# Channel attention: ten 32 x 32 diagonal blocks with tokens on partitions in place of eight, on one Trainium2 core

## The chip, the cores and the metric

The kernel runs on one core of a Trainium2 chip. The metric is the device time of one execution in microseconds (us). A core has a matrix engine (TensorE, "PE" in the profile, with its weight loads as "PEld"), a vector engine (DVE), a scalar engine (ACT), a general engine (POOL) and a queue engine for transfers (SP). Each runs its own instructions strictly in order and waits for the others by semaphores: an instruction that has to wait holds back everything behind it on its engine.

## The reference, cut to what matters

The input has 8 x 1024 tokens of 256 numbers. The first layer is an attention over the *channels* of one token: every token has 16 heads of 64 channels, and the score of channel q against channel k is the product of two numbers.

```python
Q = (x @ Wq + bq).reshape(b, s, H, C) * inv_sqrt_c      # H = 16, C = 64
K = (x @ Wk + bk).reshape(b, s, H, C)
V = (x @ Wv + bv).reshape(b, s, H, C)
scores = jnp.einsum('bshq,bshk->bshqk', Q, K)           # 64 x 64 for each token and head
scores = jnp.where(mask, -inf, scores)                  # mask: k > q
w = jax.nn.softmax(scores, axis=-1)
attn = jnp.einsum('bshqk,bshk->bshq', w, V)
x = layernorm(x + attn.reshape(b, s, 1024) @ Wo + bo)
```

A second layer (an ordinary attention over positions and a mixture of experts) follows. The change doesn't touch it.

## The kernel before, in words

`phase_a` holds the first layer. The 8192 tokens are cut into 64 tiles of 128 (t = 0 to 63), and the loop body of a tile has eight steps, c = 0 to 7. Step c treats four heads (g = c % 4) for one half of the tile's tokens (ww = c // 4). The order of all instructions is written out by hand (`manual_schedule`), in the loop and in five tables (`head`, `fill_a`, `middle`, `between`, `fill_b`) that say which side job is put at which place of which step.

The 64 x 64 triangle of a head is cut into an upper 32 x 32 triangle, a lower one and a full square between them. There are two ways to compute them.

- **On TensorE.** `scores(t, c, which)` forms the products with matmuls into PSUM tiles `pair` (L418), the mask being added by a matmul with `sel` and `late` (L407). ACT takes the exponential into an `e` tile (L433). `sums(t, c, which)` multiplies `e` with the values `V`, which also hold a column of ones, into the PSUM tile `sum` (L453, L463), and ACT copies that into `S` (L479), from where POOL's transfers bring it into `nd` (L489). `which` 0 and 1 are the upper triangle with the square, 64 columns for each head, `which` 2 is the lower triangle, 32 columns.
- **With tokens on partitions.** For the channels `own` = T0 to T0 + TC, DVE multiplies (`token_scores`, L536), POOL subtracts the row's maximum (`token_less`, L544), ACT takes the exponential (`token_exp`, L550, L553), DVE weighs with the values and adds up (`token_weigh`, L561, L563, L564; `token_sums`, L573). A triangle is halved again and again: squares of 16 (parts A and B), 8 (part C), 4, 2, 1 and the diagonal (part F). `invert(t, 1)` adds the results to `nd` (L584, L589) and takes the reciprocal (L590); `divide` multiplies (L594). Before the change these channels are those of heads 6 to 9: both triangles of four heads, eight blocks. TensorE computes only the square of these heads.

Other places that the steps below speak of:

- `proj_k`, `proj_q`, `proj_v` (L288, L330, L299): the projections of the next tile, at steps 0 and 1, 2 and 3, 4 and 5. They write the PSUM tile `ps`, which has one buffer: TensorE can't start a projection before DVE has read the last one (L289, L331, L306). The reads are called k0, k1, q0, q1, v0, v1 here.
- `sum` has one PSUM buffer too: the matmuls of a `sums` wait until ACT has emptied the one before. `pair` has three.
- `token_v` (L497) transposes values into the right half of `ps` at step 6; `output` puts the product with `Wo` into its left half (L632) at steps 6 and 7; DVE adds the residual (`r`, L637). `token_v_out` (L502) is ACT's copy of the transposed values into `vt`. It stands at step 7, ahead of the S copy of `sums(t, 6, "inner")`, and its semaphore is that of DVE's `r`.
- `build` issues the transfers into `R` and `L` (L370 on POOL, L376 on SP). `gather` is a small memset on POOL (L384, "event") that waits for them, and the matmuls of `scores` wait for the memset. On POOL it stands behind `token_less` of parts A and B at step 1, and behind that of part C at step 5. `token_less` A is made to wait for DVE's scans of the next tile (`extrema`, L342, L344).
- `spread_v` (L320) lays the values out for TensorE.
- The transfer `nd<-S` after step 2 (L489, on POOL's queue) waits until DVE's `divide(t, 1)` has read `nd`.

Of the kernel before, what the change touches and what calls it, by code (L numbers as in the profile page):

```python
# [165 lines left out]
def phase_a(tc, a, ident, x1_d, norm_scalars, share, view):  # L166
# [11 lines left out]
    HT = 4  # L178
    TC = HT * C1
    T0 = (H1 - HT) // 2 * C1  # L180
    own = slice(T0, T0 + TC)
    levels = {"A": [(16, 0, 4)], "B": [(16, 4, 4)], "C": [(8, 0, 16)], "F": [(4, 0, 32), (2, 0, 64), (1, 0, 128), (0, 0, 256)]}
    inner = {1: (2, 3), 2: (0, 1)}
    chunk = [0, 1, 2, 5, 6, 7, 3, 4]
    slot = {c: s for s, c in enumerate(chunk)}
    with (
# [29 lines left out]
        for to, of, n in ((0, 0, 3), (3, 5, 3), (6, 3, 2)):  # L216
            nc.scalar.dma_start(bv[:, to : to + n], bv_c[:, of : of + n], allow_slow_non_contiguous=True)
# [22 lines left out]
        for n, big in (("hi", 3e38), ("lo", -3e38)):  # L240
            lim[n] = wp.tile([P, HH], FP, name=f"lim_{n}")
# [11 lines left out]
        NV = 2 * H1 - HT  # L253
# [21 lines left out]
        nc.gpsimd.memset(Ss[1][:, :, :2, 0:32], 0.0)  # L275
# [37 lines left out]
        def spread_v(t, ww, half):  # L313

            src = state["vT", t].rearrange("p i (w u a b) -> p i w u a b", w=2, u=4, a=4)
            for qd in (2 * half, 2 * half + 1):
                at, n = (H1, (H1 - HT) // 2) if qd % 2 else (0, H1 // 2)
                V = Vs[ww][:, at : at + 2 * n].rearrange("p (i r) u (a b) -> p i r u a b", r=2, a=4)
                for aa in range(4):
                    nc.vector.tensor_copy(  # L320
                        V[32 * aa : 32 * aa + 32, :, qd // 2, :, aa, 0:4],
# [67 lines left out]
        def scores(t, c, which):  # L389
# [6 lines left out]
            heads = range(2 * which, 2 * which + 2) if which < 2 else range(4)  # L396
            n = 64 if which < 2 else 32
            g = c % 4
            free = inner.get(g, ()) if which == 2 else ()
            at = 0 if which < 2 or 0 not in free else 256  # L400
            width = 256 if free else 512
            masked = [h for h in heads if h not in free]
            for x, h in sorted(enumerate(heads), key=lambda xh: xh[1] not in free):
                if h == masked[0]:
                    for u in range(4):
                        pr = slice(32 * u, 32 * u + 32)
                        nc.tensor.matmul(  # L407
                            bank[u][:, at : at + width].rearrange("p (n i) -> p n i", i=n)[:, :, 0:32],
                            sel[pr].rearrange("p a j -> p (a j)"),
                            late[pr, None, :].to_broadcast([32, width // n, 32]),  # L410
# [4 lines left out]
                jb = 0 if which < 2 or h in free else 1  # L415
                for u in range(4):
                    pr = slice(32 * u, 32 * u + 32)
                    one = nc.tensor.matmul(  # L418
                        bank[u][:, x * 4 * n : (x + 1) * 4 * n].rearrange("p (b i) -> p b i", i=n),
                        Lt[pr, 2 * (h0 + h) + jb].rearrange("p a j -> p (a j)"),  # L420
                        R[pr, :, h0 + h, 64 - n :],
                        start=h in free,
                        stop=h in free or h == masked[-1],
# [8 lines left out]
            for i in range(2):  # L432
                nc.scalar.activation(es[i], pair[i], AF.Exp)  # L433
# [1296 lines left out]
```

## Time and profile before

| what | value |
|---|---|
| median of 3 runs | 4629.45 us (4629.16 to 4637.17) |
| the profiled execution, its own time | 4629.18 us |
| its span, first to last instruction | 4627.5 us |
| mean granted TensorE clock | 0.979 |
| the 64 tiles of `phase_a` | 57 to 3850 us of the span |
| one tile, from one `turn` (L603) to the next, 2003.80 to 2063.04 us | 59.24 us |
| DVE busy over the span | 3708.1 us (80%) |
| ACT busy over the span | 3563.6 us (77%) |
| POOL busy over the span | 3353.0 us (72%) |

Busy time of an engine includes time in which nobody waits for it. A line of the timeline has the start, the duration, the engine, the line of the kernel, the operation, what it writes and reads, how many instructions are merged in it, and in brackets how long its engine was idle before it and what ended that. Matmuls overlap; the time that a group of them takes on TensorE is read from its start to the start of the next group.

### The profile page before, as it was taken

How to read it: one execution, taken by the hardware profiler on the slowest of the kernel's cores; microseconds unless marked ns; L12 is line 12 of the kernel's file. 1: busy time of each engine (PE TensorE's matmuls, PEld its weight loads, DVE VectorE, ACT ScalarE, POOL GpSimd, SP SyncE). 2: the span in 40 equal slices, each digit the busy share in tenths (PEclk: the TensorE clock that was granted, in tenths of full speed). 3: DMA queues.
4: the chain of work that ended last, by engine and by line, in shares of the span. 5: the costliest groups of instructions: out<-in, count | busy, mean ns of one | idle time of the engine just before them, and what ended most of it. 6: DMA issues, size and time to landing. Idle time of an engine off the chain costs nothing.

```text
span 4627.5 us, 169371 instructions
## 1 busy us (share of the span) xinstructions
PE 4381.9 (95%) x70232; PEld 2971.7 (64%) x70232; DVE 3708.1 (80%) x6686; ACT 3563.6 (77%) x5015; POOL 3353.0 (72%) x5672
## 2 busy tenths in 40 slices
PE   7999999999999999999999999999999998888785
PEld 4666666666666666666666666666666665555563
DVE  6888888888888888888888888888888885677778
ACT  5888888888888888888888888888888885444344
POOL 6878887887788788778877887888788784133446
PEclk9999999999999999999999999999999999999897
DMA  2222222222222222222222222222222222232553
GB/s 81 53 50 55 51 53 52 54 53 53 52 53 55 52 55 54 52 53 51 53 52 54 53 53 53 53 54 54 52 54 53 52 51 70 59 80 70 142 160 115
DMA packets 521272, 285.66 MB, mean 62 GB/s; under 512 B 373425, under 2 KB 439345, under 8 KB 520497
## 3 DMA queue, kind: packets, MB, share of 16 engines
q1 hardware_dynamic: 378466, 113.23, 12.5%
q0 software_dynamic: 139264, 159.69, 11.1%
q8 instruction: 550, 9.01, 0.8%
q10 hardware_dynamic: 2768, 1.91, 0.2%
q14 instruction: 224, 1.84, 0.1%
HBM read 72.84 MB, written 33.85 MB: 23 GB/s over the span
## 4 chain that ended last, share of the span: by engine, by line
PE 66%; DVE 14%; POOL 5%; SPq 5%; issue 4%; DMA 3%; ACT 3%; POOLq 0%; DVEq 0%; ACTq 0%
PE pair L418 19%; PE sum L453 12%; PE sum L463 8%; PE ps L299 6%; PE pair L407 5%; PE ps L330 5%; SPq L376 4%; PE ps L632 4%; DVE s L564 2%; POOL s L544 2%; DMA L<-k 2%; PE ps L288 2%; PE pair L603 1%; ACT s L1044 1%; DVE V L320 1%
## 5 line engine op out<-in xcount | busy, mean ns | idle before, releaser
L433 ACT ACTIVATE e<-pair 128x1024 f32<-128x1024 f32 x2560 | 2482.0, 1022 | 508.3 <-PE pair L418 477.0
L418 PE MATMUL pair<-R,L 32*128 32x128 f32 (+1 forms) x28672 | 1401.7, 319 | 22.0 <-POOL event L384 20.3
L489 POOL DMA_DIRECT2D nd<-S x2048 | 973.1, 483 | 517.0 <-ACT e L433 351.8
L418 PEld LDWEIGHTS pair<-R,L 32*128 32x128 f32 x28672 | 1096.7, 186 | 139.2 <-POOL event L384 75.4
L370 POOL DMA_DIRECT2D R<-qm x2048 | 988.6, 490 | 9.9 <-issue 5.0
L453 PE MATMUL sum<-e,V 128*32 128x256 f32 x12288 | 965.4, 386 | 5.9 <-ACT S L479 5.6
L463 PE MATMUL sum<-e,V 128*32 128x128 f32 x16384 | 783.1, 274 | 0.2 <-ACT S L479 0.2
L463 PEld LDWEIGHTS sum<-e,V 128*32 128x32 f32 x16384 | 496.2, 110 | 404.3 <-ACT e L433 96.2
L544 POOL TENSOR_TENSOR s<-s,qm 128x1024 f32<-128x1024 f32 (+2 forms) x320 | 486.9, 1537 | 132.3 <-DVE lo L344 129.0
L479 ACT COPY S<-sum 128x512 f32<-128x512 f32 (+1 forms) x1024 | 551.8, 539 | 37.0 <-PE sum L463 37.0
L320 DVE COPY V<-vT 32x128 f32<-32x128 f32 (+1 forms) x2048 | 449.3, 219 | 26.2
L590 DVE RECIPROCAL att<-nd 128x384 f32<-128x384 f32 (+1 forms) x192 | 438.0, 2281 | 12.5 <-DMA nd<-S 10.1
L564 DVE TENSOR_TENSOR s<-s,vt 128x1024 f32<-128x1024 f32 (+2 forms) x320 | 409.7, 1280 | 11.1
L76 POOL TENSOR_SCALAR ve<-mv 128x1 f32<-128x1 f32 x128 | 85.0, 664 | 449.6 <-DVE mv L74 431.6
L453 PEld LDWEIGHTS sum<-e,V 128*32 128x32 f32 x12288 | 305.1, 109 | 154.2 <-issue 64.4
L407 PE MATMUL pair<-late,sel 32*128 32x256 bf16 (+1 forms) x5120 | 399.3, 298 | 4.0 <-ACT e L433 4.0
L306 DVE TENSOR_TENSOR vT<-ps,bv 128x512 f32<-128x512 f32 x128 | 87.7, 685 | 342.9 <-PE ps L299 342.9
L536 DVE TENSOR_TENSOR s<-k,qm 128x1024 f32<-128x1024 f32 (+2 forms) x320 | 324.5, 1031 | 0.0
L563 DVE TENSOR_REDUCE part<-s 128x64 f32<-128x1024 f32 (+3 forms) x320 | 301.8, 943 | 8.3 <-ACT s L550 8.3
L299 PE MATMUL ps<-xT,wv 128*128 128x128 f32 x2048 | 273.0, 289 | 25.6 <-DVE qm L331 24.8
L299 PEld LDWEIGHTS ps<-xT,wv 128*128 128x128 f32 x2048 | 248.2, 198 | 69.0 <-issue 38.5
L573 DVE TENSOR_REDUCE part<-s 128x64 f32<-128x1024 f32 (+3 forms) x320 | 287.9, 932 | 2.2
(253 smaller groups left out, 5673.9 us busy)
## 6 DMA issues: line engine op xcount, KB each, us to landing
R<-qm POOLq DMA_DIRECT2D x2048, 32.0 KB, 2.0
nd<-S POOLq DMA_DIRECT2D x2048, 32.0 KB, 1.9
L<-k SPq DMA_DIRECT2D x4088, 8.0 KB
rows_d<-yx SPq DMA_DIRECT2D x32, 512.0 KB
xT<-in_xT SPq DMA_DIRECT2D x64, 128.0 KB
xr<-in_x SPq DMA_DIRECT2D x64, 128.0 KB
x_d<-x1o SPq DMA_DIRECT2D x64, 128.0 KB
w<-in_w SPq DMA_DIRECT2D x32, 256.0 KB
```

The costliest lines, as they stand in the source:

```text
L299: nc.tensor.matmul(ps[:, i * P : (i + 1) * P], w["v"][:, c, chunk[ch] * P : (chunk[ch] + 1) * P], xT_of[t][:, c, :], start=c == 0, stop=c ...
L320: nc.vector.tensor_copy(V[32 * aa : 32 * aa + 32, :, qd // 2, :, aa, 0:4], src[32 * qd : 32 * qd + 32, :n, ww, :, aa, :],)
L370: moved.append((None, nc.gpsimd.dma_start(R[:, b, s, b, :], q[:, b, s, cols])))
L407: nc.tensor.matmul(bank[u][:, at : at + width].rearrange("p (n i) -> p n i", i=n)[:, :, 0:32], sel[pr].rearrange("p a j -> p (a j)"), late ...
L418: one = nc.tensor.matmul(bank[u][:, x * 4 * n : (x + 1) * 4 * n].rearrange("p (b i) -> p b i", i=n), Lt[pr, 2 * (h0 + h) + jb].rearrange(" ...
L433: nc.scalar.activation(es[i], pair[i], AF.Exp)
L453: nc.tensor.matmul(dst[32 * u : 32 * u + 32], Vs[ww][:, v, u, :], e[u // 2][:, u % 2, x * 256 : (x + 1) * 256].rearrange("p (b i) -> p b i ...
L463: nc.tensor.matmul(dst[32 * u : 32 * u + 32], Vs[ww][:, v if alone else H1 + v, u, :], e2[u // 2][:, u % 2, h * P : (h + 1) * P].rearrange ...
L479: nc.scalar.copy(S[:, :, at : at + 2, i0:].rearrange("p b h i -> p h b i"), ps[:, : 8 * (C1 - i0)].rearrange("p (h b i) -> p h b i", h=2, ...
L489: nc.gpsimd.dma_start(tok[:, b, s, (h0 - G) * C1 : (h0 + G) * C1], Sx[:, 4 if s else b, b, :])
L544: one = nc.gpsimd.tensor_tensor(s, s, m, ALU.subtract)
L564: nc.vector.tensor_tensor(s, s, v[:, :, None, :].to_broadcast([P, nb, w, w]), ALU.mult)
```

## The change

Two more blocks are computed with tokens on partitions: the lower triangle of head 5 and the upper triangle of head 10. `own` is now channels 352 to 671 (TC = 320, not 256). On TensorE head 5 loses its lower triangle, and head 10 only keeps its square and its lower triangle. Which blocks a call of `scores` and `sums` treats is read from the table `plan`. Since the two heads of a `sums` can now have different widths, its copy into `S` is made in two pieces where they do.

Two of the ten blocks lie in other rows of the transposed values than the eight did, so `token_v_more` transposes two strips of 32 columns more, into the unused right half of the `sum` tile of step 6, with two copies by ACT behind it. To make room in memory, `vt` and `xr` now have one buffer (pool `op`) where they had two (`xp`), and the limits of the scans (`lim`) are of 16 bits.

```diff
-    HT = 4
-    TC = HT * C1
-    T0 = (H1 - HT) // 2 * C1
+    T0, TC = 352, 320
     own = slice(T0, T0 + TC)
-    levels = {"A": [(16, 0, 4)], "B": [(16, 4, 4)], "C": [(8, 0, 16)], "F": [(4, 0, 32), (2, 0, 64), (1, 0, 128), (0, 0, 256)]}
+    nb = TC // 32
+    levels = {
+        "A": [(16, 0, nb // 2)],
+        "B": [(16, nb // 2, nb // 2)],
+        "C": [(8, 0, 2 * nb)],
+        "F": [(4, 0, 4 * nb), (2, 0, 8 * nb), (1, 0, 16 * nb), (0, 0, TC)],
+    }
+    both_heads = ((0, 0, 64, True), (1, 0, 64, True))
+    last_heads = ((2, 0, 64, True), (3, 0, 64, True))
+    whole = {0: both_heads, 1: last_heads, 2: tuple((h, 1, 32, True) for h in range(4))}
+    plan = {
+        0: whole,
+        1: {0: both_heads, 2: ((0, 1, 32, True), (2, 0, 32, False), (3, 0, 32, False))},
+        2: {
+            1: ((2, 0, 32, False), (3, 0, 64, True)),
+            2: ((0, 0, 32, False), (1, 0, 32, False), (2, 1, 32, True), (3, 1, 32, True)),
+        },
+        3: whole,
+    }
     inner = {1: (2, 3), 2: (0, 1)}
-    chunk = [0, 1, 2, 5, 6, 7, 3, 4]
+    chunk = [0, 1, 5, 6, 7, 2, 3, 4]
...
-            lim[n] = wp.tile([P, HH], FP, name=f"lim_{n}")
+            lim[n] = wp.tile([P, HH], BF, name=f"lim_{n}")
...
             es = spare.pop(0)
             for i in range(2):
-                nc.scalar.activation(es[i], pair[i], AF.Exp)
-            state["e", t, c, which] = es
+                nc.scalar.activation(es[i][:, :, :at], pair[i][:, :, :at], AF.Exp)
+            state["e", t, c, which] = es, starts
...
-            nc.scalar.copy(
-                S[:, :, at : at + 2, i0:].rearrange("p b h i -> p h b i"),
-                ps[:, : 8 * (C1 - i0)].rearrange("p (h b i) -> p h b i", h=2, b=4),
-            )
+            to = G * (g % 2) + heads[0]
+            pieces = [(0, 2)] if spans[0][1] == spans[1][1] else [(0, 1), (1, 1)]
+            for x, nh in pieces:
+                start, width = spans[x]
+                nc.scalar.copy(
+                    S[:, :, to + x : to + x + nh, C1 - width :].rearrange("p b h i -> p h b i"),
+                    ps[:, start : start + 4 * nh * width].rearrange("p (h b i) -> p h b i", h=nh, b=4),
+                )
+            if alone and c == 6 and t + 1 < NT:
+                token_v_more(t + 1, ps, 2 * P)
...
-            n = TC // P
-            for i in range(n):
-                nc.tensor.transpose(ps[:, (2 + i) * P : (3 + i) * P], state["vT", t][:, HID // P - n + i, :], ident)
-            state["vt", t] = xp.tile([P, TC], FP, name="vt")
+            for i in range(2):
+                nc.tensor.transpose(ps[:, (2 + i) * P : (3 + i) * P], state["vT", t][:, HID // P - 2 + i, :], ident)
+            state["vt", t] = op.tile([P, TC], FP, name="vt")
             state["pv", t] = ps
 
+        def token_v_more(t, ps, at):
+
+            for x, (ch, r) in enumerate(((2, slice(96, 128)), (5, slice(0, 32)))):
+                nc.tensor.matmul(
+                    ps[:, at + 32 * x : at + 32 * x + 32],
+                    state["vT", t][:, slot[ch], :],
+                    ident[:, r],
+                    start=True,
+                    stop=True,
+                )
+            for x in range(2):
+                nc.scalar.copy(
+                    state["vt", t][:, (TC - 32) * x : (TC - 32) * x + 32], ps[:, at + 32 * x : at + 32 * x + 32]
+                )
+
         def token_v_out(t):
-            nc.scalar.copy(state["vt", t], state["pv", t][:, 2 * P : 2 * P + TC])
+            nc.scalar.copy(state["vt", t][:, 32 : TC - 32], state["pv", t][:, 2 * P :])
...
-            xr = xp.tile([P, D], FP, name="xr")
+            xr = op.tile([P, D], FP, name="xr")
```

In the built program the first matmul of `token_v_more` waits on ACT's semaphore for the S copy of the same `sums` call, and the copy `token_v_out` still waits for DVE's `r`. The order of the jobs in the five tables is unchanged.

More of the change, by code (lines that the diff above doesn't have):

```diff
@@ L395, in scores @@
             bank = [pair[u // 2][:, u % 2, :] for u in range(4)]
[L396 to L403, printed above, removed]
+            work = plan[c % 4][which]
+            n = max(w[2] for w in work)
+            starts, at = {}, 0
+            for h, jb, m, mask in work:
+                starts[h] = at
+                at += 4 * m
+            fill = [starts[w[0]] for w in work if w[3]]
+            masked = [w[0] for w in work if w[3]]
+            a0, a1 = fill[0], fill[-1] + 4 * n
+            for h, jb, m, mask in sorted(work, key=lambda w: w[3]):
                 if h == masked[0]:
@@ L414, in scores @@
                         )
-                jb = 0 if which < 2 or h in free else 1
                 for u in range(4):
@@ L837, in phase_a @@
         token_v(0, pps.tile([P, 512], FP, name="ps"))
+        token_v_more(0, state["pv", 0], 0)
         token_v_out(0)
```

67 lines of the change are left out of this document (29 added, 38 removed).

## The prediction

> **What bounds the kernel now.** I read the page's busy line and slices first, then the list of waits, then the timelines of one tile engine by engine.
>
> ```profile
> PE 4381.9 (95%) x70232; PEld 2971.7 (64%) x70232; DVE 3708.1 (80%) x6686; ACT 3563.6 (77%) x5015; POOL 3353.0 (72%) x5672
> PE   7999999999999999999999999999999998888785
> ```
>
> In the slices of the 64 tiles TensorE has no gap: a tile costs the 59.24 us of its matmuls. The list of waits (who waits, for whom: us in total, times, longest) shows how near the others are:
>
> ```profile
> DVE vT L306 <- PE ps L299: 342.9, 67, 6.3
> DVE k L289 <- PE ps L288: 236.5, 63, 4.0
> ACT vt L502 <- DVE r L637: 35.8, 62, 1.3
> ```
>
> DVE has slack at two places only, 5.4 us a tile before v1 and 3.7 us before k1. Between these it works without a pause, and at `r` ACT already waits for it in nearly every tile. DVE's timeline from v1 to `r`:
>
> ```profile
> 2010.65 0.69 DVE L306 TENSOR_TENSOR vT<-ps,bv 128x512 f32<-128x512 f32 x1 [4.11 <-PE ps L299]
> ...
> 2020.22 1.22 DVE L564 TENSOR_TENSOR s<-s,vt 128x1024 f32<-128x1024 f32 x1
> 2021.48 1.22 DVE L573 TENSOR_REDUCE part<-s 128x128 f32<-128x1024 f32 x1
> 2022.80 0.43 DVE L637 TENSOR_TENSOR r<-ps,xr 128x256 f32<-128x256 f32 x1
> ```
>
> All engines around that place:
>
> ```profile
> 2022.62 0.65 PE L463 MATMUL sum<-e,V 128*32 128x128 f32 x16
> 2023.20 0.29 PE L407 MATMUL pair<-late,sel 32*128 32x256 bf16 x4
> 2023.26 0.37 ACT L502 COPY vt<-ps 128x256 f32<-128x256 f32 x1 [0.45 <-DVE r L637]
> 2023.53 0.38 ACT L479 COPY S<-sum 128x256 f32<-128x256 f32 x1
> 2024.29 0.64 PE L453 MATMUL sum<-e,V 128*32 128x256 f32 x8
> ```
>
> TensorE goes from the inner sums straight to the next scores at 2023.20. ACT empties `sum` meanwhile, by 2023.91, and TensorE wants it again at 2024.29. Two more places without slack, from the timelines of POOL, PE and DVE:
>
> ```profile
> 2039.65 0.09 POOL L384 MEMSET event<- 1x1 f32 x1
> 2039.80 0.73 PE L418 MATMUL pair<-R,L 32*128 32x128 f32 x16 [0.16 <-POOL event L384]
> 2048.76 0.69 DVE L331 SCALAR_TENSOR_TENSOR qm<-ps,bias 128x512 f32<-128x512 f32 x1
> 2049.77 1.98 PE L330 MATMUL ps<-wq,xT 128*128 128x512 f32 x4
> ```
>
> The event comes when the scores of step 2 need it, and q0 is read 0.4 us before TensorE wants `ps` for q1.
>
> **What TensorE saves.** From starts of groups in the timeline: the sums of one head take 0.46 us with 256 columns (2018.17 to 2018.63) and 0.22 us with 128; the scores of two heads with 256 take 0.97 us (0.485 each), of four with 128 0.99 us (0.25 each); four mask matmuls take 0.22 us with 512 columns, 0.12 with 256, so about 0.06 with 128. For half a tile, head 5 loses one scores block and part of a mask (0.25 + 0.06 = 0.31) and one sums block (0.22); head 10 goes from 256 to 128 columns: 0.235 + 0.06 = 0.30 in scores, 0.24 in sums. That is 1.07 us, 2.14 us a tile. `token_v_more` adds two matmuls, four records in the profile's way of counting: at 0.12 us each as with the 128x128 weights of `proj_v` (16 in 1.98 us) 0.5 us, as the two transposes L497 (0.27 us together) 0.27; I take 0.4. ACT gains about as much as it loses: eight exponentials get 256 elements shorter (1059 ns at 1024, 845 at 768 in L550's rows: 0.21 us each, 1.7 us), against 0.9 us for parts A, B, C and F, 0.1 for split copies and some 0.5 for two small ones.
>
> **What DVE and POOL get.** Rows by form: a reduction takes 1210, 676 and 407 ns with 1024, 512 and 256 elements, a product 681, 419 and 286 with 512, 256 and 128: 1.04 ns an element. So an instruction on part A, B or C (1024 to 1280) gets 0.27 us longer, one on 512 elements 0.13, on 256 0.07, on 128 0.03. POOL's subtraction (1945, 1124 and 728 ns) gets 0.41 us longer on A, B or C. Reciprocals: 2545 ns for 384, 1753 for 256, 6.2 ns an element; the two outer ones get 0.2 us shorter, the inner one 0.4 longer. In all some 5.6 us more on DVE in a tile, on 48.9 busy (3128 us in 64 tiles); below 59, so DVE isn't the bound by its sum. What counts is where it falls.
>
> **The path, step by step** ("+" is later than in the tile shown, with v1 as zero).
> 1. From v1 to `r`: weighing F 0.13 + 0.07 + 0.13 + 0.07 + 0.03 + 0.07 = 0.50, weighing and summing C 3 x 0.27 = 0.80, the spread -0.03: 1.27 us. DVE waited 0.1 us here before `r` (0.29 on average: 18.3 us over 64 tiles), so `r` is 1.1 late and ends at 2024.33.
> 2. The new matmuls sit behind the S copy, this one behind the copy into `vt`, and that behind `r`. 2024.33 + 0.03 + 0.27 (start of L502 to start of the copy) + 0.38 + 0.05 for the handover = 2025.06; plus 0.4 for the matmuls themselves: TensorE takes up the scores of step 7 at 2025.46, not 2023.20: +2.26. What it had saved since v1 (0.22 + 0.30 + 0.24) is spent waiting.
> 3. Step 1 saves 0.31: k1 at +1.95. DVE reaches the scans at +1.1 + 0.54 (scores A, B) - 0.24 (reciprocal, division) = +1.4, POOL's A and B add 0.82: the event at +2.2. The scores of step 2 start at +2.2.
> 4. From k1 to q0 DVE has more: sums F 0.20, the additions to `nd` 0.13 + 5 x 0.07, reciprocals 0.2, division 0.05: 0.93. q0's read ends at 2049.36 + 1.95 + 0.93 = 2052.24. TensorE would be ready for q1 at 2049.77 + 2.2 - 0.22 - 0.30 - 0.24 = 2051.21; it starts at 2052.3: +2.5.
> 5. Scores F 0.30, weighing A and B 4 x 0.27: q1's read ends at 2056.64 + 4.25 = 2060.9, as v0 wants `ps` at 2061.0. Step 5 saves 0.31: v1 at **+2.2 us**. DVE (sums A, B and scores C: +5.0) is through its scans at 2069.6 and waits for v1 at 2072.0, so step 1 starts afresh in every tile.
>
> The event of step 6 is covered: POOL's transfers `nd<-S` wait for the division (+2.88), F adds 0.45 and C 0.41: the event, at 2069.12 in the next tile, comes at 2072.9, 0.9 us too late for its scores (2069.79 + 2.2), but TensorE would stand before the new matmuls in that time anyway; with that cover gone it would cost 0.9. The single buffers cost nothing: `vt` is overwritten by a copy that waits for `r`, behind its last reader on DVE, and `xr` is loaded at step 2, 25 us after `r` has read the last one (SP's queue then holds no transfer up). The 16-bit limits lie between no gain and 0.5 us a scan (from 1.21 us to the 0.68 us of a product of that size); I take none, since TensorE comes to the event at +1.95 anyway.
>
> The sum: `token_v_more` stands in the loop 63 times, 63 x 2.2 = 139; 4629.2 + 139 = 4768 us. The profiled execution (4629.18) is the median's (4629.45). This case's own ends: without the stalls of steps 3 and 4, 2.26 - 1.38 (all that TensorE saves behind the stall) = 0.88 us a tile, 4685; with weighing A and B slowed by POOL (L564's mean is 1582 ns against 1.22 us alone, twice 0.36 before q1), 0.4 more in step 1 and 0.1 in step 2, 3.4 us a tile, 4843.
>
> **Rivals.** *The clock drops (slower still).* TensorE stands still once a tile, from 2022.44 (2023.20 - 0.76) to 2025.06, 2.6 us, less what step 6's event takes of it: 1.7 to 2.6 us. The windows of the trace (span, busy times by engine, granted clock, transfers):
>
> ```profile
> 3980.00:3982.50 2.50, 0.00 (x0) 0.00 (x0) 0.27 (x2) 2.50 (x15) 0.00 (x0) 1.00 0.01 3
> 3865.00:3867.50 2.50, 1.94 (x20) 1.40 (x12) 2.43 (x7) 0.88 (x1) 0.00 (x0) 0.50 0.00 0
> ```
>
> A gap of 2.97 us (ended 3982.69) left the clock at 1.00; one of 2.16 us among tiny matmuls (ended 3864.07) was followed by 7 us at about half, some 3.4 us lost. In a tile 1.4 of these would go into stalls that steps 3 and 4 charge anyway, so 2 us: 4768 + 126 = 4894 if in every tile, 4810 in a third. Against it: the gap is 0.4 us or more shorter than the harmless one. The Trainium skill, "TensorE: Matmul & The Clock Gate", section "Why this matters for your kernels", warns of idle gaps above about 3 us between bursts, after which the clock halves. By it the gap is harmless and the sum stays 4768; by the row at 3865 it need not be.
>
> *TensorE goes on setting the time (faster).* For it: 95% busy, idle time on the others. If DVE were not late at `r`, a tile would cost 1.16 (step 2 without lateness) - 1.38 = -0.22 us, 4615; with the wait of the new matmuls hidden too, -2.14 + 0.4 = -1.74 us, 4520. It decides from a lateness below 0.22 us; against it are 1.27 us of work on an engine that had 0.1 to 0.3 us there.
>
> *A balance.* Lateness near 0.2 us: no change.
>
> **How the numbers follow.** The path 0.75 (4685 to 4843), the clock 0.15 (4800 to 4900), TensorE 0.07, balance 0.03. Three runs agree within 0.2%, about what a measurement here can tell from no change (9 us). Predicted 4768, range 4685 to 4880; faster 0.07, same 0.03, slower 0.90.
>
> **What would show it.** In the changed profile: TensorE idle 1.7 to 2.6 us a tile, released by the S copy at step 7; ACT's wait for `r` up from 0.6 to above 1 us a tile; a tile of 61 to 62 us; TensorE waiting for DVE before q1; DVE still waiting before v1. Wrong would be: no idle time of TensorE at step 7, a tile under 59 us, or a clock below 1 within the tiles.

## The result, and the profile after

| | before | changed |
|---|---|---|
| time, us (medians of the runs compared) | 4629.89 | 5005.35 (4992.07 to 5028.6, 4 runs) |
| ratio, with its 95% interval | 1 | 1.0813 (1.077 to 1.0855) |
| predicted, us | | 4768 (4685 to 4880) |
| mean granted clock of the profiled run | 0.979 | 0.956 |
| a tile from v1 to v1, median (mean), us | 59.23 (59.99) | 65.07 (65.79) |
| of it v1 to `r` | 12.15 (12.35) | 15.55 (15.53) |
| `r` to k1 | 16.87 (16.79) | 18.12 (18.79) |
| k1 to v1 | 30.21 (30.85) | 30.65 (31.47) |

The kernel got slower as predicted, but by 375 us instead of 139, which is beyond the predicted range. The last four rows come from the timelines of DVE: the starts of its reads v1, `r` and k1, and the medians of their distances, with the means over 61 tiles in brackets (medians of parts need not add up to that of the whole; the means do). From the first v1 to the last the profiled run takes 354 us longer than the one before (4127.8 and 3773.9), of 363 for the whole span, so the tiles hold the loss. The profiled run of the changed kernel took 4992.07 us. Its busy line:

```profile
PE 4438.5 (89%) x68440; PEld 2985.4 (60%) x68440; DVE 4106.3 (82%) x6686; ACT 3517.0 (70%) x5271; POOL 3553.9 (71%) x5672
```

Records of TensorE fell by 1792 and its busy time rose, so the records got longer on average. DVE's instructions are as many as before, and their busy time rose by 398 us: 6.2 us a tile, where the prediction had 5.6; but 2.0 of the 6.2 are one product that has only 0.13 us more to do, as is seen below. The list of waits (who waits, for whom: us in total, times, longest):

```profile
DVE vT L322 <- PE ps L315: 209.7, 66, 5.5
...
PE pair L435 <- POOL event L400: 115.8, 57, 3.7
...
PE sum L517 <- ACT S L491: 106.0, 63, 3.4
...
ACT vt L530 <- DVE r L665: 88.4, 62, 3.2
PE ps L346 <- DVE qm L347: 83.0, 62, 1.4
```

TensorE now stands still in three places of a tile: before the scores that need POOL's event (2.0 us each; 20.3 us in all before), before the new matmuls (1.7 us, in every tile) and before q1 (1.3 us). DVE still waits before v1, 3.2 us a tile. Where v1 to `r` grew is seen in the timeline of one tile, DVE and POOL together (start, duration, engine, line):

```profile
2048.63 2.42 POOL L572 TENSOR_TENSOR s<-s,qm 128x1280 f32<-128x1280 f32 x1
2048.93 0.69 DVE L322 TENSOR_TENSOR vT<-ps,bv 128x512 f32<-128x512 f32 x1 [2.97 <-PE ps L315]
2049.54 0.81 DVE L591 TENSOR_REDUCE part<-s 128x160 f32<-128x640 f32 x1
2050.38 4.52 DVE L592 TENSOR_TENSOR s<-s,vt 128x640 f32<-128x640 f32 x1
2050.98 0.09 POOL L400 MEMSET event<- 1x1 f32 x1
2051.03 1.27 POOL L368 TENSOR_TENSOR qm<-qm 128x512 f32<-128x512 f32 x1
2052.25 1.27 POOL L369 TENSOR_TENSOR lo<-lo,qm 128x512 f32<-128x512 f32 x1
2053.48 0.72 POOL L641 TENSOR_TENSOR xr<-xr,bo 128x256 f32<-128x256 f32 x1
...
2065.47 0.41 DVE L665 TENSOR_TENSOR r<-ps,xr 128x256 f32<-128x256 f32 x1
```

The first product of weighing F (L592) takes 4.52 us. It takes 0.82 us where nothing runs on POOL beside it (one tile here, all tiles of e1). It ends at 2054.90, 0.70 us after POOL has finished its last elementwise instruction (2054.20), as if it had only been let in then. Over all tiles its mean is 3160 ns. In 63 tiles it met POOL's run, and it always ended 0.69 to 0.79 us after the end of one of POOL's instructions: in 31 tiles after the last (L641; in 22 of them it had come as early as L572), in 16 after L369 and in 16 after L368. Where it got in ahead of another, that one became longer: L641 then took 1.30 to 1.41 us instead of 0.72, L369 1.85 to 1.96 instead of 1.27. The reduction ahead of it (L591), beside the same POOL instruction, took its usual 0.81. The same place before the change:

```profile
2011.87 0.72 POOL L613 TENSOR_TENSOR xr<-xr,bo 128x256 f32<-128x256 f32 x1
2011.97 1.17 DVE L564 TENSOR_TENSOR s<-s,vt 128x512 f32<-128x512 f32 x1
```

There only the last of POOL's instructions was left when the product came, and it cost half a microsecond (1.17 against 0.69 alone). In these two tiles POOL's run ended 1.94 us after v1 began, and ends 5.27 us after it now. How the lateness at `r` reaches TensorE, from the timelines of DVE, ACT and PE in the same tile:

```profile
2065.92 0.37 ACT L530 COPY vt<-ps 128x256 f32<-128x256 f32 x1 [1.48 <-DVE r L665]
2066.19 0.38 ACT L491 COPY S<-sum 128x256 f32<-128x256 f32 x1
2066.62 0.63 PE L517 MATMUL sum<-ident,vT 128*128 128x32 f32 x4 [1.72 <-ACT S L491]
2067.18 0.29 PE L425 MATMUL pair<-late,sel 32*128 32x256 bf16 x4
```

That is the predicted chain, link by link: `r`, the copy into `vt`, the S copy, the new matmuls, and only then the scores of step 7. The four records of the new matmuls take 0.56 us from start to start (predicted 0.4). The third thing is in the timeline of PE and in windows of the same tile (span; busy times of PE, PEld, DVE, ACT, POOL; granted clock; transfers):

```profile
2051.12 0.73 PE L435 MATMUL pair<-R,L 32*128 32x128 f32 x16 [2.23 <-POOL event L400]
...
2052.33 2.36 PE L473 MATMUL sum<-e,V 128*32 128x256 f32 x24
```

```profile
2053.00:2055.00 2.00, 2.00 (x24) 0.97 (x20) 2.00 (x2) 1.61 (x3) 2.00 (x4) 0.50 0.11 12
...
2066.00:2069.00 3.00, 2.38 (x44) 1.80 (x48) 2.97 (x4) 1.43 (x5) 2.19 (x3) 1.00 0.00 0
```

After 2.23 us of standing still for the event the clock is at half for 3.41 us; after 1.72 us it is not. Summed over windows of 5 us through the tiles, (1 - granted clock) x 5 us is 133 us after the change and 14 before. What that costs is read from tiles side by side. One stretch of half clock takes 1.71 us of full clock away. From `r` to k1, 41 tiles have none and take 18.11 to 18.12 us, 14 have one and take 19.67 to 19.74, and 6 have two and take 21.15 to 21.27. The windows of two such stretches:

```profile
555.37:575.12 19.75, 18.52 (x288) 11.15 (x289) 12.89 (x28) 14.14 (x21) 14.58 (x22) 0.91 0.16 36
621.22:639.33 18.11, 17.06 (x296) 10.41 (x288) 12.75 (x27) 14.03 (x21) 14.59 (x22) 1.00 0.17 39
```

That is about 41 us in all, an estimate from these 20 tiles. Another 73 of the 133 us lie between v1 and `r`, where DVE waits for nobody in the changed kernel (0.00 us a tile), so there the slow clock delays nothing at `r`.

### The profile page after: what moved, and what is told of

Same layout as the page of the kernel before. It is cut to its first block, busy times and chain, and to the rows that moved or that the text cites. A ratio compares the mean times of both kernels' runs of the same rounds, so it can differ in the third digit from the quotient of the medians.

```text
span 4990.3 us, 166234 instructions
## 1 busy us (share of the span) xinstructions
PE 4438.5 (89%) x68440; PEld 2985.4 (60%) x68440; DVE 4106.3 (82%) x6686; ACT 3517.0 (70%) x5271; POOL 3553.9 (71%) x5672
## 3 DMA queue, kind: packets, MB, share of 16 engines
q14 instruction: 226, 1.85, 0.1%
## 4 chain that ended last, share of the span: by engine, by line
PE 43%; DVE 38%; ACT 6%; issue 5%; POOL 4%; DMA 3%; SPq 0%; DVEq 0%; ACTq 0%; POOLq 0%
PE sum L473 12%; PE pair L435 11%; DVE s L592 8%; DVE att L618 5%; PE ps L315 5%; DVE V L336 4%; DVE part L591 4%; PE ps L304 4%; DVE nd L617 3%; PE pair L425 3%; DVE part L601 2%; PE ps L346 2%; ACT e L450 2%; POOL nd L503 2%; ACT S L491 1%
## 5 line engine op out<-in xcount | busy, mean ns | idle before, releaser
L450 ACT ACTIVATE e<-pair 128x1024 f32<-128x1024 f32 (+1 forms) x2560 | 2375.9, 982 | 700.5 <-PE pair L435 682.4
L473 PE MATMUL sum<-e,V 128*32 128x256 f32 (+1 forms) x27648 | 1330.4, 331 | 8.8 <-ACT S L491 3.4
L572 POOL TENSOR_TENSOR s<-s,qm 128x1280 f32<-128x1280 f32 (+2 forms) x320 | 635.7, 2001 | 62.8 <-DVE lo L360 61.6
L491 ACT COPY S<-sum 128x512 f32<-128x512 f32 (+2 forms) x1152 | 547.5, 490 | 149.4 <-PE sum L473 145.7
L592 DVE TENSOR_TENSOR s<-s,vt 128x1280 f32<-128x1280 f32 (+2 forms) x320 | 594.3, 1857 | 11.0
L336 DVE COPY V<-vT 32x128 f32<-32x128 f32 (+2 forms) x2048 | 439.4, 215 | 60.3 <-PE sum L473 34.1
L618 DVE RECIPROCAL att<-nd 128x352 f32<-128x352 f32 (+1 forms) x192 | 437.9, 2281 | 11.3 <-DMA nd<-S 9.1
L425 PE MATMUL pair<-late,sel 32*128 32x256 bf16 (+2 forms) x5120 | 392.2, 291 | 3.6 <-ACT e L450 3.6
L591 DVE TENSOR_REDUCE part<-s 128x80 f32<-128x1280 f32 (+3 forms) x320 | 366.0, 1144 | 7.2 <-ACT s L578 7.2
L564 DVE TENSOR_TENSOR s<-k,qm 128x1280 f32<-128x1280 f32 (+2 forms) x320 | 370.6, 1175 | 0.0
L601 DVE TENSOR_REDUCE part<-s 128x80 f32<-128x1280 f32 (+3 forms) x320 | 351.8, 1131 | 2.2
```

Source lines behind the costliest of these rows:

```text
L336: nc.vector.tensor_copy(V[32 * aa : 32 * aa + 32, :, :, aa, 0:4], src[32 * qd : 32 * qd + 32, :n, ww, :, aa, :],)
L450: nc.scalar.activation(es[i][:, :, :at], pair[i][:, :, :at], AF.Exp)
L473: nc.tensor.matmul(dst[32 * u : 32 * u + 32, :, width - n :], Vs[ww][:, H1 * jb + v, u, :], e[u // 2][:, u % 2, starts[h] : starts[h] + 4 ...
L491: nc.scalar.copy(S[:, :, to + x : to + x + nh, C1 - width :].rearrange("p b h i -> p h b i"), ps[:, start : start + 4 * nh * width].rearra ...
L572: one = nc.gpsimd.tensor_tensor(s, s, m, ALU.subtract)
L591: nc.vector.tensor_reduce(token_place(level, 1), s, AX.X, ALU.add)
```

## The experiments

Four theories. **W**: the wait of the new matmuls (with `r` only a little late) is most of the loss. **C**: the late event of step 6 and the slow clock behind it are. **P**: POOL's run of elementwise instructions holds DVE's product, so `r` is several microseconds late. **P'**, formed after the first experiment: it holds any product or copy of DVE that stands behind v1, not this one product alone. Every ratio is against the kernel before, measured beside the run on the same chip. That kernel's median was 4675 us beside e1 to e4, 4633 beside e5 to e8 and 4684 beside e9 to e12, so only ratios and differences from it are compared. What makes it differ seems to lie behind the tiles: from the last v1 to the end, the profiles of e1 to e4 and e9 to e12 take 867 to 884 us, all others 810 to 829. So the stretches of a tile can be compared across the whole table. They are medians:

| run | us (before) | ratio (95%) | v1 to `r` | `r` to k1 | k1 to v1 | clock loss, us |
|---|---|---|---|---|---|---|
| before | | 1 | 12.15 | 16.87 | 30.21 | 14 |
| changed | 5005.35 (4629.89) | 1.0813 (1.077 to 1.0855) | 15.55 | 18.12 | 30.65 | 133 |
| e1 | 5153.95 (4674.98) | 1.1033 (1.101 to 1.1056) | 16.71 | 19.68 | | 178 |
| e2 | 4920.1 (4674.98) | 1.0528 (1.051 to 1.0545) | 15.45 | 16.64 | 30.75 | 67 |
| e3 | 5145.45 (4674.98) | 1.0999 (1.0981 to 1.1018) | 15.52 | 20.68 | 30.64 | 189 |
| e4 | 4768.67 (4674.98) | 1.0202 (1.0185 to 1.0219) | 12.23 | 18.19 | 29.98 | 22 |
| e5 | 4627.31 (4633.11) | 0.9986 (0.9976 to 0.9996) | | | | |
| e6 | 4805.53 (4633.11) | 1.0376 (1.0355 to 1.0397) | 14.79 | 16.53 | 30.55 | 43 |
| e7 | 4897.2 (4633.11) | 1.0566 (1.0549 to 1.0584) | 13.57 | 18.12 | 30.65 | 82 |
| e8 | 4753.32 (4633.11) | 1.0251 (1.0234 to 1.0268) | 12.2 | 16.77 | 32.58 | 48 |
| e9 | 4837.77 (4683.58) | 1.0325 (1.0311 to 1.0339) | 12.5 to 14.6, 16.8 to 17.8 | 17.68 | 28.72 | 94 |
| e10 | 4773.51 (4683.58) | 1.0192 (1.0177 to 1.0208) | 12.5 | 16.64 | 30.65 | 38 |
| e11 | 4617.61 (4683.58) | 0.986 (0.9845 to 0.9875) | | | | 0 |
| e12 | 5108.28 (4683.58) | 1.0909 (1.0892 to 1.0926) | 15.57 | 19.68 | | 116 |

### e1: DVE's copies ahead of the product

```diff
-            5: [("", token_weigh, "F"), ("+", spread_v, 0, 0), ("+", spread_v, 0, 1)],
+            5: [("+", spread_v, 0, 0), ("+", spread_v, 0, 1), ("", token_weigh, "F")],
```

> The changed kernel with one change of order on DVE: at step 5 the spread of the values (16 copies, 3.6 us) goes ahead of the weighing of part F. Theory P (POOL in DVE's way): from the read of v1 to r the changed kernel takes 15.55 us in the median tile (12.15 before, 13.25 predicted), because the product of part F on 640 elements runs into POOL's unbroken run of part C, two products and the residual's bias, and takes 3.2 us in the mean. Behind the spread it begins some 5.1 us after v1, when POOL's run is nearly over, and takes 0.8 to 1.2 us: v1 to r falls to 13.0 to 13.6, the tile by 2 to 2.5 us, the kernel to 4840 to 4890 us. Theory C (the late event at step 6 and the slow clock behind it make the loss): DVE is not what is waited for, the time stays at 4980 to 5030. Theory W (the wait of the new matmuls behind the S copy makes the loss): r is earlier, so that wait shrinks, and the time falls as in P, but then the next run below removes the same time without touching DVE.

Slower than the changed kernel, not faster. The product fell to 825 ns as P says. But the copies now stood where it had stood (timeline of e1, DVE and POOL):

```profile
2031.59 7.41 DVE L336 COPY V<-vT 32x128 f32<-32x128 f32 x16
...
2035.17 0.72 POOL L641 TENSOR_TENSOR xr<-xr,bo 128x256 f32<-128x256 f32 x1
```

Sixteen copies of 0.22 us are 3.6 us; they took 7.41. The first three took 2.49, 1.20 and 0.68 us, and each ended about 0.1 us after one of POOL's instructions (L368, L369, L641); the other thirteen, behind POOL's run, took their usual 0.2 to 0.26. On average the copies lost 3.5 us where the product had won 2.4, so `r` came 1 us later still. The times that P and C had named were both missed. P in its narrow form fell; P' was put in its place.

### e2: the new matmuls ahead of the S copy

```diff
+            if alone and c == 6 and t + 1 < NT:
+                token_v_more(t + 1, ps, 2 * P)
             to = G * (g % 2) + heads[0]
...
             if alone and c == 6 and t + 1 < NT:
-                token_v_more(t + 1, ps, 2 * P)
+                token_v_more_out(t + 1, ps, 2 * P)
```

> The changed kernel with the two matmuls of token_v_more ahead of the S copy of the same call (their two copies stay behind it), so that TensorE doesn't wait for ACT there. Theory P: TensorE goes on to the scores of step 7 at once, but then needs the sum buffer 1.1 us later, and that still hangs on r: r to k1 falls from 18.12 to about 16.9 us, the tile by 1.2 us, the kernel to about 4930 (4900 to 4955). Theory W: the whole wait (106 us in total) and the matmuls behind it (35 us) go: 4860 or less. Theory C: as P, or less than 40 us, since the event comes no earlier.

The two copies into `vt` stay where they were; only the matmuls no longer wait for the S copy. `r` to k1 falls by 1.5 us, below its value before, and about 130 of the 375 us go (245 us over the kernel before, ratio 1.0528 against 1.0813). More than P had expected and less than W; v1 to `r` is as long as ever. So the wait of the new matmuls is about a third of the loss, the slow clock behind it included.

### e3: the event ahead of part C

```diff
-            5: [("", token_less, "C")],
...
-            5: [("+", products, 1), ("-", residual_bias)],
+            5: [("", token_less, "C"), ("+", products, 1), ("-", residual_bias)],
```

> The changed kernel with POOL's subtraction of part C behind the event of step 5 instead of ahead of it, so that the scores of step 6 no longer wait for those 2.4 us. Theory C: TensorE's wait for the event (116 us in total) goes, and with it most of the time lost to the clock (in the tiles 1 minus the granted clock adds up to 135 us, 14 before): 4800 to 4870. Theory P: that wait goes, but DVE's product still meets POOL and r is as late as before, so the time moves into the wait of the new matmuls, which grows from 1.7 to over 3 us a tile; only the clock's share that isn't lost again there is won: 4930 to 5010.

C falls: the wait for the event is gone and the kernel is slower still. P missed the time as well, since it had expected 4930 to 5010 us; it was right on where the wait would go. The list of waits and the timeline of PE in e3:

```profile
PE sum L517 <- ACT S L491: 287.5, 63, 5.8
```

```profile
2046.10 0.63 PE L517 MATMUL sum<-ident,vT 128*128 128x32 f32 x4 [4.58 <-ACT S L491]
...
2046.79 1.93 PE L435 MATMUL pair<-R,L 32*128 32x256 f32 x16
```

TensorE now stands in one piece of 4.6 us at the new matmuls, where it had 2.0 and 1.7 us in the changed kernel, and the same scores that took 1.04 us there in the changed kernel take 1.93 behind it: the clock sum rises to 189 us. So on TensorE the event's wait was covered, as the prediction had said. v1 to `r` stays, since POOL's run is no shorter.

### e4: the new matmuls alone, in the kernel before

```diff
+            if alone and c == 6 and t + 1 < NT:
+                token_v_more(t + 1, ps, 2 * P)
             if last and g % 2 == 1:
```

> The kernel before with the two added matmuls and their two copies by ACT alone, at the place and with the wait that the change gives them; what they make is not used. All other work is as before. Step 2 of the prediction: r ends when it did, TensorE takes up the scores of step 7 1.16 us later, 63 times: 73 us, less what the next tile gives back; 4680 to 4710. Theory W: that wait is most of the change's loss: 4800 or more. Theory P: as step 2.

The strips go into a tile that nothing reads. `r` to k1 gets 1.32 us longer, where the prediction has 1.16 for this step without lateness. The kernel takes 94 us more, above the 50 to 80 that were expected; 63 x 1.32 are 83. One line of its list of waits shows it:

```profile
PE sum L508 <- ACT S L479: 61.0, 63, 2.1
```

### e5: single buffers and 16-bit limits alone, in the kernel before

```diff
-            lim[n] = wp.tile([P, HH], FP, name=f"lim_{n}")
+            lim[n] = wp.tile([P, HH], BF, name=f"lim_{n}")
...
-            state["vt", t] = xp.tile([P, TC], FP, name="vt")
+            state["vt", t] = op.tile([P, TC], FP, name="vt")
...
-            xr = xp.tile([P, D], FP, name="xr")
+            xr = op.tile([P, D], FP, name="xr")
```

> The kernel before with the single buffers of vt and xr and the 16-bit limits alone. The prediction put them at nothing: within 0.2% of the kernel before (9 us), v1 to r 12.15 us and r to k1 16.87 us as there. A loss of 30 us or more would mean that one of them makes a wait.

Ratio 0.9986 (0.9976 to 0.9996), the tile at 59.24 us: they cost nothing.

### e6: a longer run on POOL, eight blocks

To e5's kernel two additions on POOL that nobody waits for, on a tile `pad` of their own, behind the addition of the bias:

```diff
+        def longer(t):
+            nc.gpsimd.tensor_tensor(pad, pad, pad, ALU.add)
+            nc.gpsimd.tensor_tensor(pad[:, :512], pad[:, :512], pad[:, 512:], ALU.add)
...
-            5: [("+", products, 1), ("-", residual_bias)],
+            5: [("+", products, 1), ("-", residual_bias), ("", longer)],
```

> The kernel before with the single buffers and 16-bit limits, and with two more additions on POOL, of 1024 and of 512 elements on a tile of their own, behind the residual's bias of step 5; TensorE's, ACT's and DVE's work is that of eight blocks, and no new matmuls are there. POOL's run behind the event of step 5 so ends about 3.2 us later, as it does in the changed kernel. Theory P': any product or copy that DVE has behind the read of v1 is held until POOL's run is through. Then part F's product goes from 1.2 us to 3.5 to 4.5, v1 to r from 12.15 to 14.5 to 15.5 us, and the kernel takes 150 to 270 us more than the kernel before. Theory C (event and clock): the event isn't touched, less than 40 us more. If the loss came from the longer DVE work of ten blocks itself: less than 40 us more.

v1 to `r` grows by 2.64 us though DVE does nothing more, and the kernel loses 172 us. The first product rose less than expected (mean 2512 ns); the small ones behind it took the rest (timeline of e6, DVE and POOL):

```profile
2030.18 1.21 POOL L620 TENSOR_TENSOR xr<-xr,bo 128x256 f32<-128x256 f32 x1
...
2031.17 2.36 DVE L571 TENSOR_TENSOR s<-s,vt 128x256 f32<-128x256 f32 x1
2031.36 1.88 POOL L508 TENSOR_TENSOR pad<-pad 128x1024 f32<-128x1024 f32 x1
2033.32 1.34 POOL L509 TENSOR_TENSOR pad<-pad 128x512 f32<-128x512 f32 x1
2033.45 1.36 DVE L568 TENSOR_TENSOR part<-part,vt 128x128 f32<-128x128 f32 x1
```

The product of 256 elements takes 2.36 us instead of 0.42 and ends 0.29 us after POOL's first addition; the one of 128 takes 1.36 instead of 0.28 and ends 0.15 us after the second. A DVE product can thus be let in between two of POOL's instructions, as in 32 of 63 tiles of the changed kernel; in 22 others it was passed over every time.

### e7: POOL's run taken away, ten blocks

```diff
-            5: [("+", products, 1), ("-", residual_bias)],
+            5: [],
```

> The changed kernel without POOL's two products of the second half and without the residual's bias at step 5, the 3.2 us that lengthen POOL's run there; so it leaves out the product of the maxima with q for heads 8 to 15 and the addition of bo. Theory P': v1 to r falls from 15.55 to 12.9 to 13.6 us (the prediction had 13.25), and of the changed kernel's loss against the kernel before (375 us) 130 to 220 us go. Theory C: the event is as late as before, less than 40 us go. If the ten blocks' DVE work itself were what makes r late: v1 to r stays above 15 us.

Row of e7's product by form (count, busy us, mean ns, idle before):

```profile
L592 DVE TENSOR_TENSOR s<-s,vt 128x640 f32<-128x640 f32 x64 | 70.9, 1108 | 2.2
```

From 3160 to 1108 ns, and v1 to `r` from 15.55 to 13.57, near the predicted 12.15 + 1.1 = 13.25. That is the median; the mean is 14.31, of which DVE works 13.21 us and waits 1.10, for ACT's exponential and for TensorE. With the hold gone the slow clock shows at `r`: the 31 tiles without it between v1 and `r` take 13.3 us on average, the 29 with one stretch of it 15.25. 111 of the 375 us go, a little less than expected. `r` to k1 and k1 to v1 don't move at all: the wait for the event (114.5 us) and the one before q1 stay.

### e8, e9, e10: ten blocks in another order

e8 takes together what the runs had shown: the new matmuls ahead of the copy (e2), all of `token_less` behind the events, POOL's products and DVE's maxima of the second half moved behind `r`'s work, and the outer reciprocal from step 1 to step 3.

```diff
         head = {
-            1: [("", token_less, "A"), ("", token_less, "B")],
-            5: [("", token_less, "C")],
         }
...
+            1: [("", token_less, "A"), ("", token_less, "B")],
...
-            5: [("+", products, 1), ("-", residual_bias)],
-            6: [("--", normal), ("+", maxima, 1)],
-            7: [("", token_sums, "C")],
+            5: [("", token_less, "C"), ("-", residual_bias)],
+            6: [("--", normal)],
+            7: [("", token_sums, "C"), ("+", products, 1)],
...
-            1: [("-", invert, 2), ("-", token_sums, "F"), ("-", invert, 1), ("-", divide, 1)],
+            1: [("-", token_sums, "F"), ("-", invert, 1), ("-", divide, 1)],
...
-            3: [("", token_sums, "A"), ("", token_sums, "B"), ("", token_scores, "C"), ("-", divide, 2)],
+            3: [("", token_sums, "A"), ("", token_sums, "B"), ("", token_scores, "C"), ("-", invert, 2), ("-", divide, 2)],
...
-            7: [("+", token_scores, "A"), ("", invert, 0), ("+", token_scores, "B"), ("", divide, 0)],
+            7: [("+", token_scores, "A"), ("", invert, 0), ("+", token_scores, "B"), ("", divide, 0), ("+", maxima, 1)],
```

> The changed kernel with five changes of order and nothing left out: the two new matmuls ahead of the S copy; POOL's subtractions of parts A, B and of part C behind the events of steps 1 and 5; the products of the second half at step 7 behind its event, with DVE's maxima behind them at the end of step 7; the outer reciprocal of step 1 behind the weighing of step 3. Theory P': POOL's run behind v1 is 2.5 us shorter, r at most 13.5 us after v1; q0 is read 2.3 us earlier, so TensorE's wait before q1 (1.3 us a tile) goes; the events come earlier. A tile of 58 to 61 us: between 90 us less and 120 us more than the kernel before. Theory C: the same, since the events are early here too; this run doesn't tell the two apart but shows whether ten blocks can pay.

The product is down to 880 ns, v1 to `r` to 12.2 us, `r` to k1 to 16.77, and the kernel to +120 us, at the upper edge of what was expected. What is left has moved: the later reciprocal makes TensorE wait for `att` at `turn`. One line of e8's list of waits:

```profile
PE pair L635 <- DVE att L626: 92.7, 57, 4.1
```

e9 puts `turn` one step later as well, so that it doesn't wait:

```diff
-            4: [("-", turn), ("+", extrema, 1)],
-            5: [("", token_weigh, "F"), ("+", spread_v, 0, 0), ("+", spread_v, 0, 1)],
+            4: [("+", extrema, 1)],
+            5: [("-", turn), ("", token_weigh, "F"), ("+", spread_v, 0, 0), ("+", spread_v, 0, 1)],
```

> The reordered ten blocks of the run before with one more change of order: the transposes of att (turn) one step later, at the end of step 5, since in that run TensorE waited 1.6 us a tile for the last division there. Theory P' with the path of the prediction: v1 to r 12.2 us and r to k1 16.8 us as in that run, k1 to v1 from 32.6 to 29.2 to 30.2 us, a tile of 58.2 to 59.3 us: between 70 us less and 10 us more than the kernel before.

A miss. k1 to v1 is the shortest of all, 28.72 us, so TensorE has the work for a faster tile. But v1 now comes earlier against POOL: its subtraction of part C and the addition of the bias lie beside weighing F again (product 2573 ns). And in 30 of 61 tiles POOL's products, now at step 7, hold weighing C's product too: 3.99 to 4.17 us instead of 1.49. So v1 to `r` is 12.5 to 14.6 us in 31 tiles and 16.8 to 17.8 in the others. e10 is e8 with the reciprocal back at step 1:

```diff
-            1: [("-", token_sums, "F"), ("-", invert, 1), ("-", divide, 1)],
+            1: [("-", invert, 2), ("-", token_sums, "F"), ("-", invert, 1), ("-", divide, 1)],
```

> The reordered ten blocks with the outer reciprocal back at step 1 and the transposes at step 4. P' with the path: the wait for the division at the transposes goes, the wait before q1 (1.3 us a tile) is back: k1 to v1 30.65 us as in the changed kernel, a tile of 59.5 to 60.2 us: 10 to 70 us more than the kernel before. If the two were independent of each other it would be near the run before (120 us more).

+90 us, just above what was expected, and the best order of ten blocks that was run. The medians of all three stretches are within 0.5 us of the kernel before, but ten blocks still lose 2%: the mean tile takes 61.4 us against 60.0, by 0.67 us more from v1 to `r` and 0.75 from k1 to v1.

### e11: the same order with eight blocks

The kernel before with e9's edits of the tables (they are those of e8's and e9's diffs; eight blocks need no new matmuls).

> The kernel before, eight blocks, with the changes of order of e9 that apply to it (events first, late products and maxima, late reciprocal, late transposes). TensorE has 59.2 us of matmuls a tile here and next to no idle time: within 25 us of the kernel before. If this run gains as much as e9, the order gains and not the ten blocks.

Faster than expected, and faster than both kernels: 0.986 (0.9845 to 0.9875), 66 us. The usual tile hardly changes (median 59.06 us, 59.23 in the profile of before). The mean falls from 60.0 to 59.1 and the longest from 63.8 to 59.9, which makes 60 us from the first v1 to the last, and the clock stays at full speed in all windows of the tiles, where 15 of 740 were below 0.99. What the order wins is the rare long tile. Which of its moves does it was not tried singly.

### e12: matmuls that nobody reads in TensorE's two waits

```diff
+            for x in range(32 if c == 6 and which == 2 else 0):
+                pr = slice(32 * (x % 4), 32 * (x % 4) + 32)
+                nc.tensor.matmul(
+                    bank[x % 4].rearrange("p (n i) -> p n i", i=32),
...
+            for x in range(12 if alone and c == 6 and t + 1 < NT else 0):
```

> The changed kernel with matmuls that nobody reads put into TensorE's two waits: 32 with 512 columns (1.8 us) ahead of the scores of step 6, 12 with 256 columns (1.3 us) ahead of the S copy of step 7. What is computed stays the same. In the changed kernel 1 minus the granted clock adds up to 133 us in the tiles (14 before). If those are part of the loss: they fall below 70 us, and the kernel takes 40 to 110 us less than the changed kernel, 265 to 335 us more than the kernel before. If the slow clock only falls into time that DVE sets anyway: as the changed kernel or up to 40 us slower, 360 to 420 us more than the kernel before.

Meant to keep the clock up and so to price it. The clock sum fell only from 133 to 116 us, while the filler made TensorE later. The time, 425 us over the kernel before, lies above both expected ranges, and the run prices nothing: for the clock's own share there are only the tiles side by side, as shown with the result.

## Why the prediction was right in direction and wrong in size

**The path was right.** Each link that steps 1 to 5 name is in the trace: `r` late, ACT waiting for it (88.4 us, from 35.8), the new matmuls behind the S copy, k1 late, TensorE waiting for DVE before q1 (1.3 us a tile), v1 late, DVE with slack before v1 so that each tile starts afresh. Rival "TensorE goes on setting the time" fell with the first of these: it decides from a lateness of 0.22 us, and there were several.

**Step 2** (the new matmuls wait behind S, `vt`, `r`): right. 1.16 us without lateness predicted, 1.32 in e4. From `r` to k1 step 3's saving of 0.31 comes off; 0.85 predicted, 1.25 measured by the medians; 0.16 of the 0.40 more are the matmuls themselves (0.56 instead of 0.4 us).

**Steps 3 to 5**: k1 to v1 was put 0.25 us longer and is 0.44 (0.62 by the means). DVE's extra work from k1 to q0, 0.93 us, is 0.92 (10.01 us in the tile shown, 9.09 in the one before).

**Step 1 failed: the lateness of `r` was mis-sized.** It counted DVE's own extra work, 1.27 us, less the 0.1 it had waited, made `r` 1.1 us late, and put POOL's hold of DVE's product at nothing. `r` is 3.4 us late by the medians (3.2 by the means), and 4.4 in the tile shown (16.54 against 12.15). The rest is that hold. Two things made POOL's run later: the event of step 6 was worked out to be "0.9 us too late" and called "covered", which for TensorE it was (e3), but with it POOL's products and the bias moved under DVE's weighing; and `token_less` F took 1.4 us more on POOL on average (5.3 against 3.9) where the prediction put 0.45. The prediction's own times could have shown it: its event comes at 2072.9, 0.9 us behind its v1 at 2072.0, and behind the event POOL had 3.2 us of products and bias to do. It used POOL's influence only in its upper end, with 0.4 us for step 1. That the hold does it is shown from both sides: more POOL work without any DVE work costs 2.64 us at the same place (e6), and without POOL's run DVE works 13.21 us from v1 to `r` on average (e7), where it worked 15.53 in the changed kernel and 12.18 before.

**What step 1 leaves.** A tile is 5.8 us longer by the means, not 2.2: 3.2 from v1 to `r` (1.1 predicted), 2.0 from `r` to k1 (0.85) and 0.6 from k1 to v1 (0.25). Of the 3.6 us between, 2.1 are step 1's, about 0.7 the slow clock between `r` and k1, and the rest smaller terms. So step 1 alone doesn't make the whole difference: without POOL's run (e7) the kernel still loses 264 us.

The Trainium skill, "SBUF — State Buffer", section "Who interferes with whom", states the rule that step 1 lacked: a DVE instruction with two inputs in SBUF contends with a POOL instruction that reads SBUF, copies can contend too, a reduction never does, and the loser is blocked, not slowed. This case agrees with that division and with the block: products (4.52 for 0.82 us) and copies (7.41 for 3.6) were held, the reduction beside them was not (0.81). It adds that the block can last past one instruction: in the tile shown the product waited through the rest of L572, the memset, L368, L369 and L641, 3.7 us.

**The clock** was priced as a rival at 0.15, for gaps after `r`; it came as a part of the loss instead, 133 us of reduced clock against 14. The price that the rival named per stall, 2 us, and the 42 us for "a third" of the tiles are near what the tiles side by side give, 1.6 us and 41 us in 20 of 61; that the two agree is partly luck, since `r` was far later than the rival assumed. The gap that shows it best is the one that step 6's event was said to cover. The Trainium skill, "TensorE: Matmul & The Clock Gate", section "Why this matters for your kernels", warns of gaps above about 3 us; here 2.23 us was followed by a clock of 0.50, while 1.72 us was not, and the two rows shown with the prediction had it both ways (2.16 us followed by half, 2.97 us harmless). By these rows the length of a gap alone doesn't decide. The trace of the changed kernel shows more. In its tiles the clock changes only after whole multiples of 3.41 us. Cut into such pieces, the time from 300 to 3700 us has 60 full-clock pieces right ahead of a half-clock one, with TensorE busy for at most 0.48 of each, and 861 others, with TensorE busy for at least 0.48. So it also matters how a gap falls on these pieces. The filler of e12 does not fit: there a piece that was busy for 0.86 was followed by half clock.

**A bill on TensorE**, as an estimate from the two profiles: waits for the event 95 us more, for the S copy 100 (106.0 less 5.6 that the outer sums waited for it before), before q1 83, other waits 27 (TensorE's idle time rose by 306 in all), the new matmuls 63 x 0.56 = 35, the clock 119, less 63 x 2.14 = 135 that the prediction has TensorE save: 324 of the 363 us between the two profiles. Some 40 us are not assigned. The clock's 119 is an upper bound, since the windows of low clock hold idle time too. Taken away one at a time, the wait of the new matmuls is worth 130 us (e2) and POOL's run 111 (e7); both together without further moves were not tried.

**The cost nothing** edits: right (e5).

## What to carry to other kernels

An instruction's price depends on what the other vector engine does beside it. When a step moves work in time on POOL, look in the trace at which DVE products and copies it will lie beside, and price the hold: here it was about twice the extra work itself (2.3 us against 1.27). A new write into a buffer that another engine empties inherits everything queued ahead of that engine's copy; put the write ahead of the copy, or give it a place of its own. And a wait that is "covered" for the engine that is waiting may not be so for the engine that is late: follow what stands behind the late instruction there as well. Where tiles fall into groups, a median shows only one of them: from `r` to k1 the medians show 1.25 us of the 2.0 that the means do.

## What the runs showed of the hardware

- DVE's products and copies were blocked by back-to-back elementwise instructions on POOL. A product that had been held ended a fixed time after the end of one of them: 0.69 to 0.79 us with 640 elements (changed kernel), 0.55 to 0.66 with 512 (before and e6), 0.28 to 0.29 with 256 (e6), 0.15 with 128 (e6's tile). In the changed kernel that was the last of the run in 31 of 63 tiles and an earlier one in 32. What decides which is open.
- POOL pays too: in the changed kernel the addition of the bias took 1.30 to 1.41 us instead of 0.72 where the product of 640 elements got in just ahead of it. Its subtraction on part F with 640 elements took 1990 ns on average against 1124 with 512; it fell into two groups, 2.1 us in 51 tiles and 1.3 in 9, all beside a DVE reduction and a DVE product.
- A stall of 4.58 us was followed by the same 16 matmul records in 1.93 us instead of 1.04 (e3), one of 2.23 us by 24 records in 2.36 us, where 32 like them take 1.51 at full clock.
- Scans with limits of 16 bits took as long as with 32 (1217 and 1196 ns on both kernels).
